# Two-layer perceiver block: seven block products for keys and values, and normalisation chains on VectorE

## The chip, the cores and the metric

The kernel runs on one core of one Trainium2 chip. The metric is the device time of one launch in microseconds. Lower is better. The time before is the median of three runs, 1554.78 us.

## The reference

Sixteen sequences of 64 tokens, 256 features each (x), pass through two layers of three blocks, each added to x after a layer norm. A context of 1024 rows a sequence feeds the cross-attentions.

```
x = x + cross_attention(layernorm(x), ctx_1024, mask, ...)          # layer 0, 16 heads of 16
x = x + attention over the 16 sequences, rotary, causal             # layer 0
x = x + mixture of 8 experts, top 2 (layernorm(x))                  # layer 0
x = x + cross_attention(layernorm(x), ctx_1024, bias, mask, ...)    # layer 1
x = x + attention over the 64 tokens, rotary (layernorm(x))         # layer 1
x = x + fp4_linear(silu(fp4_linear(h, gate)) * fp4_linear(h, up), down)   # layer 1, h = layernorm(x)
...
kv = context @ Wkv + bkv          # (1024 x 256) @ (256 x 512): keys, then values, of one sequence
attn = softmax(q k / 4, masked); out = attn @ v; out @ Wout + bout
...
fp4: per block of 16 elements scale = max|x| / 6, round x / scale to the fp4 grid, times scale
```

Everything is float32. The quantization of the feed-forward is done by adding and subtracting a large number of the right magnitude.

## The kernel before

Tokens lie in eight tiles of 128 rows (two sequences each), n = 0 to 7. The work goes by stages: the cross-attention of layer 0 (0 to about 530 us in the profile), the attention over sequences (to about 660), router and experts (to about 870), then layer 1, in which `cross_attention` runs again and its `after` hook starts, for each finished tile, `row_attention` and `feed_forward` as chains between the steps of the next tiles.

**Cross-attention.** The outer loop runs over 64 slots: 16 sequences b, two halves of the features dt, two halves of the keys hf. In slot i the kernel issues on PE, in this order: the scores of slot i + 2 (`scores`, L445: four matmuls of 512 columns on four row groups at once), the first part of the keys and values that are due (`project`, L361), the transposes of the exponentials of two key blocks (`transpose_keys`, L475), the second part of what is due, two more transposes, and the products with the values of slot i - 1 (`attend`, L489). VectorE adds the mask to the scores and takes their running minimum in one instruction (L456, with its read-out), ScalarE makes exponentials of 1024 columns at a time when both halves are there (L467). The transposes and products leave PSUM by copies: in odd slots by VectorE, in even ones by ScalarE (`evacuate`, L217 and L219; keys with their bias L378 and L380). In layer 1 half of the transposes of odd slots go to ScalarE too (L602).

`project` has eight steps a sequence: four for keys (L370: two matmuls of 512 columns, one for each half of the 256 contracted features), four for values (L385: four matmuls of 256 columns). Sequence b's steps are due in slots 4b - 4 to 4b - 1, two in each (L549). Every work tile in PSUM comes from one pool of seven banks (`bank`, L137, tile name psw), in turn; an eighth holds the outputs (pso).

PE's order is that of the program (`manual_schedule`). The other engines' order is set by the scheduler. Each engine runs its instructions in order. The chains (`queries`, `outputs`, and the later layers) are generators: each `yield` hands on to the next step of the slot, so that the number of yields sets how far a chain's steps lie apart in PE's order.

**Layer norm of a tile** (`layernorm_rows`, L241): statistics on VectorE, an inverse root by three Newton steps of three 128x1 operations each on GpSimd (L256 to L258), and the normalisation on GpSimd (L260). **Output projection** (`project_rows`, L297): VectorE adds the bias to PSUM (L303), GpSimd adds the result to x (L304).

**Quantization** (`fp4`, L883): absolute value on ScalarE (L890), block maximum, scale and reciprocal on VectorE (L893 to L898), product, exponent, addition and subtraction, product (L899 to L911). `feed_forward` (L1361) quantizes the normalised tile, multiplies by gate and up (L1376) in two halves of 352 columns, quantizes the two halves of h in turn, transposes (L1391) and multiplies by the down weights (L1405).

**Ahead of time.** While the middle stages run, PE fills gaps with the keys and values of layer 1 for nine sequences (`make_ahead`), from two buffers of the pool `ahead` (actx) and staging buffers (astage); the first two contexts are loaded on SP's queue with the later weights (`later`, L614). The feed-forward weights wgT, wuT, wdT (L1159) are filled during the experts' stage and are unused before.

Of the kernel before, what the change touches and what calls it, by code (L numbers as in the profile page):

```python
# [118 lines left out]
def kernel(ctx: ExitStack, tc: tile.TileContext, a: dict, out: bass.AP):  # L119
# [121 lines left out]
    def layernorm_rows(pool, n, name="xnr"):  # L241

        st = small.tile([P, 6], F32, name="bnst")
        nc.vector.bn_stats(st, x[n])
        mv = small.tile([P, 2], F32, name="mvr")
        nc.vector.bn_aggr(mv, st)
        va = small.tile([P, 1], F32, name="var")
        nc.vector.tensor_scalar(va, mv[:, 1:2], EPS, None, ALU.add)

        half = small.tile([P, 1], I32, name="half")  # L250
        nc.vector.tensor_scalar(half, va.bitcast(I32), 1, None, ALU.logical_shift_right)
        r = small.tile([P, 1], F32, name="rsd")
        nc.vector.tensor_scalar(r.bitcast(I32), half, -1.0, 1597463007.0, ALU.mult, ALU.add)
        t = small.tile([P, 1], F32, name="nwt")
        for _ in range(3):
            nc.gpsimd.tensor_scalar(t, r, va, r, ALU.mult, ALU.mult)  # L256
            nc.gpsimd.tensor_scalar(t, t, -0.5, 1.5, ALU.mult, ALU.add)
            nc.gpsimd.tensor_tensor(r, r, t, ALU.mult)  # L258
        xn = pool.tile([P, D], F32, name=name)
        made[name] = nc.gpsimd.tensor_scalar(xn, x[n], mv[:, 0:1], r, ALU.subtract, ALU.mult)  # L260
        yield
        yield
        yield
        return xn
# [32 lines left out]
    def project_rows(n, oT, w, bias):  # L297

        pm = bank()
        for c in range(KC):  # L300
            nc.tensor.matmul(pm[:, :D], oT[:, c, :], w[:, c, :], start=(c == 0), stop=(c == KC - 1))  # L301
        t = small.tile([P, D], F32, name="prow")
        nc.vector.tensor_tensor(t, pm[:, :D], bias, ALU.add)  # L303
        nc.gpsimd.tensor_tensor(x[n], x[n], t, ALU.add)  # L304


    def cross_attention(layer, wq, wkv, wo, bq, bk, bv, bo, mask, keep, bias, after, ready, arrive, idle):
        side = "right" if layer else "left"
        with ExitStack() as st:
# [83 lines left out]

            def queries(n):
# [3 lines left out]
                xn = yield from layernorm_rows(single, n, "xnq")  # L398
# [98 lines left out]
            def outputs(b):  # L497
# [38 lines left out]
                project_rows(n, oT, wo, rowbias(bo))  # L536
# [6 lines left out]
            for b in range(1, B):  # L543
                if b not in ready:
# [29 lines left out]
            with tc.manual_schedule(engines={mybir.EngineType.PE}):  # L574
# [15 lines left out]
                for i in range(len(slots) + 1):  # L590
# [5 lines left out]
                    for part in range(2):  # L596
                        for step in steps[part::2]:
                            project(*step, vector)
                        if i < len(slots):
                            b, dt, hf = slots[i]  # L600
                            for k in (4 * hf + 2 * part, 4 * hf + 2 * part + 1):
                                transpose_keys(b, dt, k, vector and (layer == 0 or part == 0))  # L602
                                advance()
# [7 lines left out]
                    if i % 4 == 0 and i // 4 + 2 < B:  # L611
                        load(i // 4 + 2)
                        if i == 4:
                            for w, source in later:  # L614
                                nc.sync.dma_start(w, source)
                            later.clear()
                    if i % 8 == 0 and i // 8 + 1 < NT:
# [54 lines left out]
    actx, ready = {}, {}  # L672
# [6 lines left out]
    for b in range(2):  # L679
        load_ahead(b, lambda w, source: later.append((w, source)))  # L680
# [202 lines left out]
    def fp4(pool, dst, src, rows, n, tag, most=None):  # L883

        nb = n // BLK
        most = most or n
        shape = [rows, nb, BLK]
        t = pool.tile([P, most], F32, name=f"t{tag}")[:rows, :n]
        t3 = t.rearrange("p (g k) -> p g k", k=BLK)
        nc.scalar.activation(t, src, AF.Abs)  # L890
        yield
        scl = pool.tile([P, most // BLK], F32, name=f"scl{tag}")[:rows, :nb]
        nc.vector.tensor_reduce(scl, t3, AX.X, ALU.max)  # L893
        nc.vector.tensor_scalar(scl, scl, 1.0 / 6.0, 1e-12, ALU.mult, ALU.max)
        rsc = pool.tile([P, most // BLK], F32, name=f"rsc{tag}")[:rows, :nb]
# [4 lines left out]
            t3, src.rearrange("p (g k) -> p g k", k=BLK), rsc.unsqueeze(2).to_broadcast(shape), ALU.mult  # L900
# [4 lines left out]
        m = pool.tile([P, most], F32, name=f"m{tag}")[:rows, :n]  # L905
# [257 lines left out]
    def quantize_weights(step, pool):  # L1163
        if step < 4:
# [9 lines left out]
            for _ in fp4(pool, q, raw, PG, n, "w"):  # L1174
# [12 lines left out]
        elif step < 6:  # L1187
# [4 lines left out]
            for _ in fp4(pool, q, raw, P, NI, "d"):  # L1192
# [15 lines left out]
    def last_layers(one):  # L1208
# [11 lines left out]
        def row_attention(n, two):  # L1220
            vz = vzs[n % 2]
            xn = yield from layernorm_rows(two, n)
# [134 lines left out]
            project_rows(n, oT, wproj, rowbias("L1_attn_b_proj"))  # L1357
# [3 lines left out]
        def feed_forward(n, two):  # L1361
            tok = slice(n * P, (n + 1) * P)
            xn = yield from layernorm_rows(two, n)
            yield from fp4(one, xn, xn, P, D, "h", NI)
# [5 lines left out]
            for g in range(2):  # L1370
                cols = slice(g * NH, (g + 1) * NH)
                pg = bank()[:, :NH]
                pu = bank()[:, :NH]
                for ps, w in ((pg, wgT), (pu, wuT)):
                    for c in range(KC):
                        nc.tensor.matmul(  # L1376
                            ps, xT[:, c, :], w[:, c, cols], start=(c == 0), stop=(c == KC - 1)
# [3 lines left out]
            yield  # L1381
            for g in range(2):
                cols = slice(g * NH, (g + 1) * NH)
                yield from fp4(one, h[:, cols], h[:, cols], P, NH, "h", NI)
            yield
            hT = one.tile([P, NCH, P], F32, name="hT")
            for g in range(0, NCH, 3):
# [12 lines left out]
            yield  # L1400
            yield
            py = bank()[:, :D]
            for j in range(NCH):
                w = min(P, NI - j * P)
                nc.tensor.matmul(py, hT[:w, j, :], wdT[:w, j, :], start=(j == 0), stop=(j == NCH - 1))  # L1405
# [107 lines left out]
```

## Time and profile before

| what | us |
|---|---|
| median of 3 runs | 1554.78 |
| lowest and highest run | 1544.31, 1555.05 |
| profiled execution | 1553.52 |
| its span, first to last instruction | 1551.8 |
| PE, VectorE, ScalarE, GpSimd busy | 1411.0, 880.4, 725.3, 285.4 |

The span is what the profile covers, and the 1.7 us beyond it lie around the first and last instruction. The profile names lines of the kernel above. A float32 matmul takes two passes on PE and shows as two records, a transpose shows as one. "x8" in a line is eight records. PEld is the load of the fixed operand of a matmul, which overlaps with PE. An operation's tile names stand as out<-in. The chain that ended last is followed back from the last instruction: each piece waits for the one before it.

### The profile page before, as it was taken

The page shows a single profiled execution, that of the slowest core. Times are in us where ns is not written, and L with a number is a line of the kernel's source. Part 1 is how long each engine was busy: PE and PEld are TensorE (multiplying, and loading weights), DVE is VectorE, ACT ScalarE, POOL GpSimd, SP SyncE. Part 2 cuts the span into 40 slices and gives each one's busy share as a digit, 9 for nine tenths or more (in the row PEclk, how much of TensorE's full clock was granted, in tenths as well). Part 3 has the DMA queues.
Part 4 walks back from the last instruction along what each step waited for, and adds up shares of the span by engine and source line. Part 5 has one row for each costly group of instructions (what it writes and reads, how often), then busy time and mean ns, then how long its engine had stood idle before and what let it go on. Part 6 is the DMA issues. An engine that isn't in the chain of part 4 may idle for free.

```text
span 1551.8 us, 32601 instructions
## 1 busy us (share of the span) xinstructions
PE 1411.0 (91%) x13488; PEld 995.0 (64%) x13488; DVE 880.4 (57%) x2325; ACT 725.3 (47%) x1339; POOL 285.4 (18%) x502
## 2 busy tenths in 40 slices
PE   4999999999999998999999787888899999999754
PEld 2667766676667655768887555565657666666542
DVE  2556665656565533365721265675767675757543
ACT  2555555555555532223221475564656465646321
POOL 4101010000000031013300134241414141311111
PEclk8999999999999999999999798888889999999876
DMA  8111110101000021377774232322101111100000
GB/s 281 59 31 35 32 59 32 35 32 59 31 28 2 35 90 70 105 260 235 234 283 147 90 117 94 118 86 74 57 14 46 46 52 49 42 5 1 5 5 3
DMA packets 53073, 119.48 MB, mean 77 GB/s; under 512 B 4877, under 2 KB 24333, under 8 KB 50621
## 3 DMA queue, kind: packets, MB, share of 16 engines
q1 hardware_dynamic: 48876, 109.93, 21.0%
q0 software_dynamic: 1648, 4.72, 1.1%
q10 hardware_dynamic: 2400, 2.76, 0.5%
q8 instruction: 106, 1.74, 0.5%
q14 instruction: 43, 0.34, 0.1%
HBM read 94.32 MB, written 23.07 MB: 76 GB/s over the span
## 4 chain that ended last, share of the span: by engine, by line
PE 73%; DVE 12%; POOL 4%; ACT 4%; DMA 3%; issue 3%; ACTq 0%; POOLq 0%; DVEq 0%; SPq 0%
PE psw L475 11%; PE psw L385 10%; PE psw L370 9%; PE psw L445 8%; PE pso L489 7%; PE psw L659 4%; PE psw L1085 4%; PE psw L1105 4%; DVE e L456 3%; PE psw L646 3%; ACT e L467 3%; PE psw L1376 2%; PE psw L1405 2%; PE psw L301 2%; DMA kd<-astage 1%
## 5 line engine op out<-in xcount | busy, mean ns | idle before, releaser
L467 ACT ACTIVATE e<-e,mn 128x1024 f32<-128x1024 f32 x256 | 291.1, 1139 | 125.3 <-DVE mn L456 125.3
L475 PEld LDWEIGHTS psw<-consts,e 128*128 128x128 f32 x2048 | 242.6, 144 | 111.6 <-issue 64.3
L475 PE MATMUL psw<-consts,e 128*128 128x128 f32 x2048 | 286.8, 280 | 10.1 <-DVE mn L456 5.7
L456 DVE CUSTOM_DVE_ANT_0 e<-psw,negb,mn 128x512 f32<-128x512 f32 x256 | 177.9, 747 | 180.0 <-PE psw L445 180.0
L456 DVE CUSTOM_DVE_ANT_0 e<-psw,negb 128x512 f32<-128x512 f32 x256 | 162.9, 686 | 87.0 <-PE psw L445 86.8
L219 ACT COPY eT<-psw 128x512 f32<-128x512 f32 x320 | 174.1, 590 | 58.3 <-PE psw L475 57.9
L445 PE MATMUL psw<-kT,qm 32*128 32x512 f32 x1024 | 167.7, 690 | 3.4 <-ACT qm L415 1.8
L489 PE MATMUL pso<-eT,v 128*32 128x128 f32 x4096 | 146.0, 286 | 0.0
L370 PE MATMUL psw<-ctxT,w_L_xattn_Wkv 128*128 128x512 f32 x256 | 125.0, 612 | 11.9 <-DMA ctxT<-in_ctxT_dram 11.9
L217 DVE COPY eT<-psw 128x512 f32<-128x512 f32 x192 | 123.0, 678 | 9.3 <-PE psw L475 9.3
L489 PEld LDWEIGHTS pso<-eT,v 128*32 128x32 f32 x4096 | 109.4, 114 | 28.0 <-issue 25.9
L385 PE MATMUL psw<-w_L_xattn_Wkv,ctxT 128*128 128x256 f32 x512 | 123.6, 385 | 0.0
L385 PEld LDWEIGHTS psw<-w_L_xattn_Wkv,ctxT 128*128 128x128 f32 x512 | 93.0, 190 | 33.7 <-issue 11.9
L370 PEld LDWEIGHTS psw<-ctxT,w_L_xattn_Wkv 128*128 128x128 f32 x256 | 44.3, 192 | 68.4 <-issue 55.1
L219 ACT COPY v<-psw 128x512 f32<-128x512 f32 x46 | 27.0, 588 | 123.8 <-PE psw L385 123.8
L304 POOL TENSOR_TENSOR x<-x,prow 128x256 f32<-128x256 f32 x24 | 17.4, 727 | 315.1 <-DVE prow L303 315.1
L659 PE MATMUL psw<-w_L_xattn_Wkv_w,actx 128*128 128x256 f32 x288 | 73.4, 409 | 0.8 <-ACT astage L653 0.8
L445 PEld LDWEIGHTS psw<-kT,qm 32*128 32x128 f32 x1024 | 49.2, 197 | 37.8 <-issue 20.2
L337 POOL TENSOR_SCALAR negb<-m 128x1024 f32<-128x1024 uint8 x16 | 16.7, 1046 | 285.8 <-DVE mn L456 172.4
L380 ACT ACTIVATE kT<-psw,colb 128x512 f32<-128x512 f32 x48 | 32.8, 687 | 75.3 <-PE psw L370 75.3
L646 PE MATMUL psw<-actx,w_L_xattn_Wkv_w 128*128 128x512 f32 x144 | 66.2, 599 | 1.3 <-DVE x L632 1.3
L659 PEld LDWEIGHTS psw<-w_L_xattn_Wkv_w,actx 128*128 128x128 f32 x288 | 58.0, 206 | 13.6 <-issue 3.8
(248 smaller groups left out, 1974.0 us busy)
## 6 DMA issues: line engine op xcount, KB each, us to landing
ctxT<-in_ctxT_dram SPq DMA_DIRECT2D x23, 1024.0 KB, 5.0
w<-in_L_ffn_w_dram SPq DMA_DIRECT2D x16, 1024.0 KB, 6.9
actx<-in_ctxT_dram SPq DMA_DIRECT2D x9, 1024.0 KB, 6.8
kd<-astage SPq DMA_DIRECT2D x36, 256.0 KB, 3.7
vd<-astage SPq DMA_DIRECT2D x36, 256.0 KB, 2.4
kT<-kd SPq DMA_DIRECT2D x9, 1024.0 KB, 6.1
v<-vd SPq DMA_DIRECT2D x9, 1024.0 KB, 5.0
ab<-in_fside_BxS_dram SPq DMA_DIRECT2D x32, 256.0 KB, 3.4
```

The source lines that it names most:

```text
L217: nc.vector.tensor_copy(dst, src)
L219: nc.scalar.copy(dst, src)
L370: nc.tensor.matmul(pm, wkv[:, c, dt * P : (dt + 1) * P], ctxT[b][:, c, cols], start=(c == 0), stop=(c == KC - 1),)
L385: nc.tensor.matmul(pm[:, j * D : (j + 1) * D], ctxT[b][:, c, (k + j) * P : (k + j + 1) * P], wkv[:, c, D : 2 * D], start=(c == 0), stop=(c ...
L445: nc.tensor.matmul(sc[g], qm[b // 2][r : r + 32, dt, b % 2, :, :].rearrange("p j q -> p (j q)"), kT[b][r : r + 32, dt, cols], start=True, ...
L456: nc.vector.tensor_tensor_reduce(out=e[:, cols], in0=sc[g], in1=negb[b][:, cols], scale=1.0, scalar=3e38 if hf == 0 else mn[b][:, 0, pr : ...
L467: nc.scalar.activation(e, e, AF.Exp, scale=-1.0, bias=mn[b][:, 1, pr : pr + 1], accum_out=sums[b][:, pr : pr + 1])
L475: nc.tensor.transpose(pt[:, g * P : (g + 1) * P], es[b, dt, g][:, k * P : (k + 1) * P], ident)
L489: nc.tensor.matmul(po[b][32 * g : 32 * g + 32, dt, :], v[b][:, k, pr * 32 : (pr + 1) * 32], e[:, g, :], start=(k == 0), stop=(k == NK - 1),)
L646: nc.tensor.matmul(pm, w1kv[:, c, dt * P : (dt + 1) * P], actx[b][:, c, cols], start=(c == 0), stop=(c == KC - 1),)
L659: nc.tensor.matmul(pm[:, j * D : (j + 1) * D], actx[b][:, c, (k + j) * P : (k + j + 1) * P], w1kv[:, c, D : 2 * D], start=(c == 0), stop=( ...
L1085: nc.tensor.matmul(ph[:, j * CAP : (j + 1) * CAP], w1[:, c, (f + j) * P : (f + j + 1) * P], xeT[:, c, :], start=(c == 0), stop=(c == KC - 1),)
```

## The change

It has two parts.

**Seven products for keys and values of layer 0**, from the third sequence on. The contracted features and the output features are each cut in two halves of 128, the 1024 keys in two halves of 512. Of the eight block products that a 2x2 by 2x2 block product takes, one is dropped by multiplying sums of blocks (the scheme of Strassen and Winograd). It is done once for keys (m = 0) and once for values (m = 1). Sums of weights are made once on GpSimd, in the space of wgT; sums of the context's blocks on GpSimd for each sequence, in the buffers actx (`sum_context`); the products are single matmuls without accumulation, of 512 columns for keys and four of 128 columns for values. Their sums are made while they leave PSUM: three VectorE operations in each of the two phases, and in the second phase two copies on ScalarE into the space of wdT and two additions on GpSimd. Partial sums lie in wuT and astage. Each phase of a sequence takes a slot, from slot 4b - 5 on: three products in the first, four in the second. Half of the transposes of odd slots now leave by ScalarE in layer 0 too. The two contexts for layer 1 are loaded at slot 59, since sums use their buffers.

**Chains on VectorE**, in layer 1: `layernorm_rows` of the row attention, of the feed-forward and of the first query does its Newton steps and normalisation on VectorE; the output bias is added to x earlier on GpSimd, so that `project_rows` is one VectorE addition; `fp4` takes the absolute value inside its maximum and so leaves ScalarE out (in the quantization of weights too); the feed-forward's halves are 384 and 320 columns, and in the last tile the second half of gate and up, the first half of the transposes and of the down product are interleaved with the quantizations.

```diff
+        if vector:
+            nc.vector.tensor_scalar(va, va, -0.5, None, ALU.mult)
+            for _ in range(3):
+                nc.vector.tensor_scalar(t, r, va, r, ALU.mult, ALU.mult)
+                nc.vector.scalar_tensor_tensor(r, t, 1.5, r, ALU.add, ALU.mult)
+            made[name] = nc.vector.tensor_scalar(xn, x[n], mv[:, 0:1], r, ALU.subtract, ALU.mult)
+            return xn
...
+        if bias is None:
+            nc.vector.tensor_tensor(x[n], pm[:, :D], x[n], ALU.add)
+            return
...
+            seven = layer == 0
+                wsum = wgT.rearrange("p c n -> p (c n)")[:, : 10 * P].rearrange("p (o m n) -> p o m n", o=5, m=2)
+                    nc.gpsimd.tensor_tensor(wsum[:, o, :, :], p0, p1, op)
+                nc.gpsimd.tensor_scalar(wsum[:, 4, :, :], w4[:, 1, :, 1, :], -1.0, 1.0, ALU.mult, ALU.mult)
...
+            def sum_context(b):
+                t = xsum[b] = ahead.tile([P, KC, SK], F32, name="actx").rearrange("p c (o k) -> p (c o) k", o=2)
+                X = ctxT[b]
+                for o, p0, p1 in (
+                    (0, X[:, 0, HK:], X[:, 0, :HK]),
+                    (1, X[:, 1, HK:], t[:, 0, :]),
+                    (2, X[:, 1, HK:], X[:, 0, HK:]),
+                    (3, t[:, 1, :], X[:, 1, :HK]),
+                ):
+                    nc.gpsimd.tensor_tensor(t[:, o, :], p0, p1, ALU.subtract)
...
+                def product(a_, x_):
+                    pm = bank()
+                    if m == 0:
+                        nc.tensor.matmul(pm, a_, x_, start=True, stop=True)
+                    else:
+                        for q in range(4):
+                            cols = slice(q * P, (q + 1) * P)
+                            nc.tensor.matmul(pm[:, cols], x_[:, cols], a_, start=True, stop=True)
...
+                if (phase, part) == (0, 0):
+                    nc.vector.tensor_copy(s1[b, m], product(W[:, 0, 0, :], X[:, 0, :HK]))
+                    p6 = product(wsum[:, 1, m, :], t[:, 1, :])
+                    nc.vector.tensor_tensor(u2[b, m], p6, s1[b, m], ALU.add)
+                elif (phase, part) == (0, 1):
+                    put(0, 0, product(W[:, 1, 0, :], X[:, 1, :HK]), s1[b, m])
+                elif (phase, part) == (1, 0):
+                    s5 = held[b, m] = ahead.tile([P, HK], F32, name="astage")
+                    p5 = product(wsum[:, 0, m, :], t[:, 0, :])
+                    nc.vector.tensor_tensor(s5, p5, u2[b, m], ALU.add)
+                    p7 = product(wsum[:, 2, m, :], t[:, 2, :])
+                    put(1, 1, p7, s5)
+                    nc.vector.tensor_tensor(u2[b, m], p7, u2[b, m], ALU.add)
+                else:
+                    put_far(0, 1, product(wsum[:, 3, m, :], X[:, 1, HK:]), held.pop((b, m)))
+                    put_far(1, 0, product(wsum[:, 4, m, :], t[:, 3, :]), u2[b, m])
...
+                if seven and b >= 2:
+                            due.setdefault(4 * b - 5 + 2 * m + phase, []).append((b, m, phase))
...
-                                transpose_keys(b, dt, k, vector and (layer == 0 or part == 0))
+                                transpose_keys(b, dt, k, vector and part == 0)
...
-        nc.scalar.activation(t, src, AF.Abs)
-        nc.vector.tensor_reduce(scl, t3, AX.X, ALU.max)
+        nc.vector.tensor_reduce(scl, s3, AX.X, ALU.max, apply_absolute_value=True)
...
+            if alone:
+                hidden(halves[0])
+                first = fp4(tiles, h[:, halves[0]], h[:, halves[0]], P, 3 * P)
+                next(first)
+                hidden(halves[1])
+                for _ in first:
+                    pass
+                turn_hidden(0)
+                py = bank()[:, :D]
+                down(0)
+                for _ in fp4(tiles, h[:, halves[1]], h[:, halves[1]], P, NI - 3 * P, 3 * P):
+                    pass
+                turn_hidden(3)
+                down(3)
```

In the diff, `put` adds a PSUM bank and a partial sum into keys (with their bias) or values on VectorE, and `put_far` copies the bank on ScalarE into wdT and adds there on GpSimd.

## The prediction

> **What bounds the kernel now.** I read the stage table first (windows of the trace; columns: stretch, its length, busy PE, weight loads, VectorE, ScalarE, GpSimd, each with a count of instructions, then granted clock, DMA share and GB/s).
>
> ```profile
> 40.00:510.00 470.00, 470.00 (x4213) 324.91 (x4211) 294.26 (x751) 254.30 (x471) 33.58 (x54) 1.00 0.11 36
> 870.00:1160.00 290.00, 245.87 (x2512) 165.98 (x2513) 185.74 (x535) 168.68 (x322) 84.84 (x148) 0.84 0.23 76
> 1160.00:1450.00 290.00, 281.38 (x2656) 198.90 (x2654) 198.79 (x553) 167.86 (x319) 75.14 (x141) 0.99 0.11 34
> 1450.00:1552.00 102.00, 53.15 (x515) 36.70 (x514) 41.05 (x110) 19.16 (x37) 14.49 (x36) 0.73 0.01 5
> ```
>
> The first row is the first cross-attention: PE never stops, VectorE is busy 63%, ScalarE 54%, GpSimd 7%. There a PE column saved is time saved, as long as nothing else comes to set the pace. The last row is the opposite: no engine is busy more than 52%, so the end is a chain of dependent steps.
>
> PE's order of time in the first stretch (start, length, engine, line, tiles, count of passes; a float32 matmul that isn't a transpose shows as two) prices the columns. I go by start to start, since ends are modelled:
>
> ```profile
> 306.96 1.99 PE L385 MATMUL psw<-w_L_xattn_Wkv,ctxT 128*128 128x256 f32 x8
> 308.79 1.04 PE L475 MATMUL psw<-consts,e 128*128 128x128 f32 x8
> ...
> 325.26 1.06 PE L405 MATMUL psw<-xTq,w_L_xattn_Wq 128*128 128x128 f32 x8
> 326.15 0.60 PE L475 MATMUL psw<-consts,e 128*128 128x128 f32 x4
> ```
>
> A step of values (four matmuls of 256 columns) takes 1.83 us just after scores and 1.73 elsewhere, so 0.433 a matmul; a step of keys (two of 512) likewise 1.82 and 1.72, so 0.86. Four matmuls of 128 columns, each with its own 128x128 weights (L405), take 0.89 us, so 0.2225.
>
> The chain that ended last shows the tail: sum on GpSimd, nine tiny GpSimd operations, normalisation on GpSimd, the absolute value on ScalarE, then quantization.
>
> ```profile
> 1513.90 0.73 POOL x L304
> 1514.66 0.44 DVE bnst L244
> ...
> 1518.90 1.29 POOLq L1509
> 1520.21 0.42 ACT th L890
> ...
> 1525.62 6.37 PE psw L1376 x12
> 1532.01 0.46 ACT h L1379
> ...
> 1542.34 1.12 PE psw L1391 x4
> 1543.45 5.21 PE psw L1405 x12
> ```
>
> **Part 1: seven products (batches 2 to 15 of layer 0).** Per batch, before: two key steps at 1.82 and two at 1.72 = 7.08; values the same with 1.83 and 1.73 = 7.12; together 14.20 us. After: keys 7 x 0.86 + 0.2 (two blocks that follow scores) = 6.22; values 28 x 0.2225 + 0.2 = 6.43; together 12.65. Saved 1.55 us a batch, 21.7 us in 14 batches.
>
> One rule of the Trainium skill speaks against this, for values become 28 matmuls of 128 columns in place of 16 of 256. TensorE: Matmul & The Clock Gate, section Back-to-back issue gap, gives about 81 ns for a pair of weight load and matmul at 128 columns and 131 at 512: a narrow matmul costs 0.62 of a wide one, not a quarter. Scaled to this kernel's 0.43 us pass of 512, 56 passes would take 56 x 0.62 x 0.43 = 14.9 us a batch against 7.1 now, a loss of 7.8 x 14 = 109 us. The row says 0.111 us a pass at 128 columns, 0.26 of a wide one, in this kernel, with new weights each time: the loads fit behind the float32 passes. I take the row.
>
> **What the sums cost elsewhere.** VectorE, per batch: 12 operations on 128x512 from PSUM where 4 were. Nearest rows: the plain copy 0.68, the one with a bias 0.75 (L378), the 128x256 sum of PSUM and SBUF 0.42 (L303), which scales to 0.68 or so. New: 10 x 0.68 + 2 x 0.75 = 8.3; gone: 2 x 0.75 + 2 x 0.69 = 2.9 and four score copies (now on ScalarE) 2.7. Net +2.7: from 294.26/470 x 31.2 = 19.5 us to 22.2 in a batch of 29.65 (31.2 is the period of the batches in the chain), 75%. ScalarE: +4 x 0.59, its four evacuations as before: 16.9 to 19.3, 65%. GpSimd: eight sums of 128x512, which neither VectorE nor PE waits for by more than a slot; L343 is that form, 1.30 us each with VectorE at 66%: +10.4 on 2.2, 42%. The block sums of the context are made two to three slots (about 20 us) ahead of their first product, and those that end in keys or values are wanted at least two slots later. Thus totals fit; order within a slot is what can hurt.
>
> **The bank ring.** Seven work banks (psw) turn round, for scores, products and transposes alike. A slot had ten; it has 11 (odd, three products) or 12 (even, four), and one more with a transposed output. Walk through an odd slot: PE 1.07 scores + 1.82 two products + 0.87 transposes + 0.96 third product + 0.87 + 1.01 attend = 6.6 us, on average 0.3 more for queries and outputs. VectorE starts its masked minima 1.16 after the slot (314.23 to 315.39 in the trace), ends them at 3.85, the first copy at 4.5, the sum at 5.15, two score copies at 6.4, with an output 7.0, third sum 7.7. The next slot's fourth scores want the bank of the second score copy (6.4), or with outputs between, that of the outputs (7.0) or the third sum (7.7). PE is there at 6.6 to 7.1. So the wait is 0 to 0.6 in an odd slot. I take 0.2 in each of the two odd slots of a batch: 14 x 0.43 = 6 us; none (0) below, and 1.8 a batch (25 us: PE waits 0.9 in every odd slot, for the third sum and the reciprocal and oT that stand about it) above. In even slots VectorE is through at 5.7, PE at 7.5: covered. PE stays above 95% busy, where the trace had clock 0.99 (1160 to 1450). Layer 0: 21.7 - 6 = 15.7 us.
>
> **Start, weights sums, moved loads.** Five GpSimd operations on weights (about 4 x 0.73 + 0.8 = 3.7 us) stand ahead of the first Newton step. GpSimd idles from 7.4 to 13.6 and again 2.3 us before 17.6; weights are there by 11.9, when PE starts. I take 0; up to 3 if that cover is gone. Two 1 MB loads for the later keys move on SP's queue from 25 us to slot 59, some 35 us ahead of their use, 6.8 us each: 0. Should they be late, the filling after the last scores shifts by as much.
>
> **Part 2: chains on VectorE (layer 1).** From the last VectorE step of a normalisation to its end GpSimd takes 1464.28 to 1468.50 = 4.2 us; on VectorE seven operations of about 0.2 (L894, 128 partitions x 22: 0.18) and one of 128x256 (0.56, L234): 2.0. Saved 2.2. The hop to GpSimd for x (0.74 + gaps) goes: 0.8. The absolute value: 0.45. So 3.4 for feed-forward and 3.0 for row attention. On the tail's path lie tile 6's feed-forward, tile 7's row attention and tile 7's feed-forward: 9.8. Then the last tile's halves. Before: 1525.62 to 1548.66 = 23.0. After: first 384 columns of gate and up 6.37 x 384/704 = 3.5; silu 0.5; VectorE back to back 9.6 (two products with h of 0.5, two quantizations of 4.3); transposes and evacuation of the second half 1.1; half of the down matmul 2.6: 17.3. Saved 5.7. Sum 15.5; tile 7's row attention also waits for tile 6's work, so I take 14 (9 if only the last feed-forward counts, 18 if clocks rise with fewer gaps).
>
> In the 580 us before, VectorE gets 16 x 2.0 = 32 us of work, 5% more, but loses waits for GpSimd and ScalarE at the head of its queue. PE there waits 15.6 us for xnq and xnr from GpSimd, 18.0 for outputs from VectorE. I take 3 us of gain (12 of gain, 8 of loss).
>
> **Sum.** 15.7 + 14 + 3 = 32.7. Span 1551.8 - 32.7 = 1519.1. The profiled execution lasted 1553.52, 1.7 around its span, and lies 1.3 below the median of 1554.78: 1522.
>
> **Rivals.**
> *The ring eats layer 0* (0.18): the upper end above, 25 us against 21.7 saved; with the 17 of layer 1: 1541, from 1533 to 1549. For it: work banks are the one resource that the change asks more of. Against it: odd slots before carried 2.7 + 2.7 + 1.4 of VectorE work, and no wait shows.
> *VectorE's sums hold PE up, slower* (0.08): the sums, which read PSUM and SBUF, cost what GpSimd's do (1.30) because the two engines hold each other up. In an odd slot the second score copy then ends at 3.85 + 2.6 + 1.28 = 7.7 and the third sum at 9.6, 8.7 on average, where PE comes at 6.85: 1.8 x 28 odd slots = 51 us lost, 21.7 and 17 saved: 1567. It decides from 1.4 us of wait a slot (38.7/28), which is a sum of about 1.13 us. For it: GpSimd goes from 7% to 42% busy. Against it: SBUF — State Buffer, section SBUF: two separate sides, ties the exclusive hold on VectorE's side to two SBUF inputs or a two-port mode, and these have one input in PSUM; and L456, which also reads PSUM and SBUF, took 0.66 us with its read-out (159.11 us in 240) where GpSimd was 7% busy and 0.67 (96.34 in 144) where it was 29%.
> *More than forecast* (0.11): no ring waits, 12 us from the freed queues: 1554.8 - 21.7 - 12 - 15.5 = 1505.
> *The change does not shorten PE's work* (inside the first rival): narrow matmuls cost more than 0.2225.
>
> **Chances.** The forecast 0.63 (own range 1508 to 1536). 1% of 1554.78 is 15.5 us, about what a measurement here can tell from nothing: faster is below 1539. The ring case lies astride it, 0.08 and 0.10. Faster 0.63 + 0.11 + 0.08 = 0.82, same 0.10, slower 0.08. Eight in ten: 1503 to 1544.
>
> **What would show it.** Right: batches 29.7 to 30.2 us apart in layer 0, PE at 98% or more, eight values passes in 0.89 us, VectorE 75% and GpSimd 42%, the tail 14 us shorter. Wrong: PE waiting for VectorE sums ahead of scores, sums far above 0.7 us, a granted clock below 1.00 there, PE waiting for context sums, or a tail that still ends in the same 23 us.

## The result, and the profile after

The changed kernel takes 1551.8 us (median of 20 runs, 1547.5 to 1556.0); the kernel before, run on the same chip beside it, 1544.3 (20 runs, 1539.1 to 1555.1). The ratio is 1.004, with a 95% interval of 1.0025 to 1.0056: 7.5 us slower by the medians (3.9 to 8.6 by the interval) where 32.7 less had been forecast. The profiled execution of before (1553.5) is among the longest of its kernel, so the two profiles, 1551.8 and 1550.0 us of span, don't show the loss in their totals. Below, totals are compared by medians, and stretches by profiles.

The stage table of the changed kernel (length, busy PE, weight loads, VectorE, ScalarE and GpSimd, granted clock, DMA share, GB/s):

```profile
40.00:510.00 470.00, 460.11 (x4581) 332.62 (x4583) 331.43 (x812) 286.36 (x536) 173.83 (x166) 1.00 0.12 41
870.00:1160.00 290.00, 235.71 (x2526) 163.20 (x2526) 191.68 (x588) 169.88 (x320) 66.14 (x91) 0.88 0.22 76
1160.00:1450.00 290.00, 270.94 (x2491) 192.78 (x2493) 192.51 (x571) 150.65 (x280) 44.33 (x65) 0.96 0.10 32
1450.00:1550.00 100.00, 66.94 (x670) 47.18 (x662) 56.14 (x166) 27.45 (x53) 5.63 (x7) 0.81 0.02 5
```

PE, never idle in the first row before, now stands still for 9.9 us of it. In the second and third rows PE lost some 10 us of busy time each at much the same length: it waits there. PE does more in the last row, 67% where it was 52%, but that is in part work which came later: slot 124 (slots are explained below) starts at 1429.8 us where it started at 1410.5.

To place the time exactly I take the start of the first masked minimum of a slot from VectorE's order of time. Slots are numbered through both cross-attentions: 0 to 63 are layer 0, 64 to 127 layer 1.

| stretch | before, us | after, us | after - before |
|---|---|---|---|
| start to slot 8 | 89.5 | 93.3 | +3.8 |
| slots 8 to 60, layer 0 | 404.9 | 399.5 | -5.4 |
| slots 60 to 64 (column attention, MoE) | 383.5 | 381.9 | -1.6 |
| slots 64 to 124, layer 1 | 532.6 | 555.1 | +22.5 |
| slot 124 to the end | 141.2 | 120.2 | -21.1 |

Profiles with the same work differ by some 3 us in the first and the last two rows and by up to 7.7 in the third (last section). The forecast had -15.7 for layer 0, -3 for slots 64 to 124, and -14 for the end.

**The loss in layer 1.** PE's longest waits for normalised rows between 870 and 1450 us, before and then after (line, what it waited for: sum in us, times, longest):

```profile
PE psw L269 <- POOL xnq L260: 12.0, 4, 3.6
```

```profile
PE psw L276 <- POOL xnq L267: 38.9, 7, 8.1
PE psw L276 <- DVE xnr L261: 12.1, 3, 5.5
```

L276 is the transposes of normalised rows, `xnq` the rows of the next query tile. One of the seven places in PE's order of time, after:

```profile
1179.29 0.60 PE L583 MATMUL psw<-consts,e 128*128 128x128 f32 x4
1184.89 0.69 PE L276 MATMUL psw<-consts,xnq 128*128 128x128 f32 x2 [5.01 <-POOL xnq L267]
1185.38 1.06 PE L583 MATMUL psw<-consts,e 128*128 128x128 f32 x4
```

PE's order is written out by hand and lets nothing pass: the other four transposes of exponentials (L583) stand behind. VectorE's queue shortly ahead of this wait:

```profile
1173.27 0.48 DVE L1035 TENSOR_TENSOR h<-th,sclh 128x320 f32<-128x320 f32 x1
1173.66 0.15 DVE L260 SCALAR_TENSOR_TENSOR rsd<-nwt,rsd 128x1 f32<-128x1 f32 x1
...
1174.86 0.41 DVE L261 TENSOR_SCALAR xnr<-x,mvr,rsd 128x256 f32<-128x256 f32 x1
1175.18 0.48 DVE L1261 SCALAR_TENSOR_TENSOR x<-g,rt_w,x 128x256 f32<-128x256 f32 x1
1175.58 0.75 DVE L564 CUSTOM_DVE_ANT_0 e<-psw,negb,mn 128x512 f32<-128x512 f32 x1
...
1180.37 0.15 DVE L253 TENSOR_SCALAR rsd<-half 128x1 int32<-128x1 int32 x1
```

and GpSimd's:

```profile
1180.64 0.34 POOL L264 TENSOR_SCALAR nwt<-rsd,var 128x1 f32<-128x1 f32 x1 [4.38 <-DVE rsd L253]
...
1183.62 1.22 POOL L267 TENSOR_SCALAR xnq<-x,mvr,rsd 128x256 f32<-128x256 f32 x1
```

The query's rows are complete only after both gathered rows are added (L1261), and these additions now come behind row attention's Newton steps (L259, L260) and the second quantization of a feed-forward (its last step is L1035), and are threaded among masked minima and copies. The last statistic (L253) is done at 1180.5. Then the query's own Newton steps, left on GpSimd, take another 4.2 us. In the kernel before, the same additions started 6.3 us after the slot's first masked minimum (1170.38, slot 100 at 1164.09) and the statistics were done at 8.5; now they start at 11.9 (slot 100 at 1163.28) and end at 17.2. The same place in the kernel before, where quantization (L893) comes behind the statistics:

```profile
1170.38 0.99 DVE L1137 SCALAR_TENSOR_TENSOR x<-g,rt_w,x 128x256 f32<-128x256 f32 x2
...
1172.46 0.15 DVE L253 TENSOR_SCALAR rsd<-half 128x1 int32<-128x1 int32 x1
...
1175.03 0.52 DVE L893 TENSOR_REDUCE sclh<-th 128x22 f32<-128x352 f32 x1 [1.41 <-ACT th L890]
```

**The gain in layer 0.** Prices are as forecast, in PE's order of time (start to start, eight passes of values 0.89 and 1.00, two of keys 0.87):

```profile
319.38 1.02 PE L444 MATMUL psw<-ctxT,w_L_xattn_Wkv 128*128 128x512 f32 x2
320.25 0.60 PE L583 MATMUL psw<-consts,e 128*128 128x128 f32 x4
...
332.26 1.16 PE L448 MATMUL psw<-w_L_xattn_Wkv,ctxT 128*128 128x128 f32 x8
333.26 1.06 PE L448 MATMUL psw<-wgT,actx 128*128 128x128 f32 x8
334.15 1.04 PE L583 MATMUL psw<-consts,e 128*128 128x128 f32 x8
```

The rule of the Trainium skill that the prediction set against this (TensorE: Matmul & The Clock Gate, section Back-to-back issue gap, with a narrow matmul at 0.62 of a wide one, and 109 us lost by the prediction's estimate) differs from the measurement, which decides: eight passes in 0.89 us against two in 0.87, or 0.26. What was not foreseen is one wait in every second batch, always of 1.3 us, for the scaled outputs:

```profile
364.95 1.04 PE L583 MATMUL psw<-consts,e 128*128 128x128 f32 x8
367.32 0.41 PE L635 MATMUL psw<-consts,osb 128*128 128x128 f32 x2 [1.33 <-DVE osb L622]
```

```profile
364.68 0.69 DVE L486 TENSOR_TENSOR wuT<-psw,astage 128x512 f32<-128x512 f32 x1
365.29 1.28 DVE L217 COPY eT<-psw 128x512 f32<-128x512 f32 x2
366.58 0.59 DVE L622 TENSOR_TENSOR osb<-psw,rec 64x128 f32<-64x128 f32 x2
```

Outputs are ready for scaling at 364.1, when PE has gone on from their transposes (L619), but stand behind a block sum (L486) and two copies on VectorE; the transposes of the result are PE's next step.

The ring of banks holds PE up too. The list of waits does not show it, since it falls inside a group of matmuls. Scores after an odd slot, before and then after:

```profile
368.29 1.14 PE L445 MATMUL psw<-kT,qm 32*128 32x512 f32 x8
369.36 1.99 PE L385 MATMUL psw<-w_L_xattn_Wkv,ctxT 128*128 128x256 f32 x8
```

```profile
322.44 1.54 PE L553 MATMUL psw<-kT,qm 32*128 32x512 f32 x8
323.91 1.98 PE L444 MATMUL psw<-actx,wgT 128*128 128x512 f32 x4
```

```profile
322.06 0.74 DVE L463 SCALAR_TENSOR_TENSOR kT<-psw,colb,astage 128x512 f32<-128x512 f32 x1
```

In the kernel before, the four matmuls of a slot's scores start within 0.02 us, and PE's next step follows 1.07 us after the first. Here the fourth starts 0.40 us behind the third, 0.06 us after the end of the slot's third sum on VectorE (L463, 322.80), whose semaphore it waits for since that sum frees its bank; the next step follows after 1.47. In two batches this happens once, and a second time with 0.22 us: 0.31 us a batch.

**The end.** The chain that ended last, after, from the last tile's sum:

```profile
1519.73 0.43 DVE x L310
...
1523.01 0.42 DVE xnr L261
...
1528.34 6.58 PE psw L1507 x16
...
1546.93 0.42 DVE prow L1568
```

From the sum behind the projection (L310, L303 before) to gate and up 8.6 us where it was 12.2, and from there to the last sum 18.6 where it was 23.1.

### The profile page after: what moved, and what is told of

Same layout as the page of the kernel before. It is cut to its first block, busy times and chain, and to the rows that moved or that the text cites. A ratio compares the mean times of both kernels' runs of the same rounds, so it can differ in the third digit from the quotient of the medians.

```text
span 1550.0 us, 33551 instructions
## 1 busy us (share of the span) xinstructions
PE 1389.2 (90%) x13796; PEld 998.2 (64%) x13796; DVE 928.9 (60%) x2509; ACT 745.7 (48%) x1373; POOL 366.2 (24%) x449
## 3 DMA queue, kind: packets, MB, share of 16 engines
q1 hardware_dynamic: 48876, 109.93, 20.9%
## 4 chain that ended last, share of the span: by engine, by line
PE 72%; DVE 15%; ACT 5%; DMA 3%; issue 3%; POOL 2%; ACTq 0%; SPq 0%; DVEq 0%; POOLq 0%
PE psw L583 11%; PE psw L553 9%; PE pso L597 7%; PE psw L444 6%; DVE e L564 5%; PE psw L448 5%; PE psw L1209 4%; ACT e L575 4%; PE psw L1229 4%; PE psw L778 3%; PE psw L380 3%; PE psw L765 3%; PE psw L395 2%; PE psw L1507 2%; PE psw L1356 1%
## 5 line engine op out<-in xcount | busy, mean ns | idle before, releaser
L583 PEld LDWEIGHTS psw<-consts,e 128*128 128x128 f32 x2048 | 240.6, 144 | 97.8 <-issue 55.4
L583 PE MATMUL psw<-consts,e 128*128 128x128 f32 x2048 | 284.5, 279 | 7.7 <-ACT e L575 5.2
L219 ACT COPY eT<-psw 128x512 f32<-128x512 f32 x384 | 208.1, 587 | 148.7 <-PE psw L583 148.4
L597 PE MATMUL pso<-eT,v 128*32 128x128 f32 x4096 | 139.0, 277 | 0.0
L217 DVE COPY eT<-psw 128x512 f32<-128x512 f32 x128 | 82.4, 682 | 3.1 <-PE psw L583 3.1
L772 ACT ACTIVATE astage<-psw,colb 128x512 f32<-128x512 f32 x36 | 24.7, 687 | 77.2 <-PE psw L765 45.3
L448 PEld LDWEIGHTS psw<-wgT,actx 128*128 128x128 f32 x448 | 53.3, 192 | 10.6 <-issue 5.3
L448 PE MATMUL psw<-wgT,actx 128*128 128x128 f32 x448 | 58.3, 278 | 0.0
L1209 PE MATMUL psw<-xeT,w 128*128 128x256 f32 x256 | 56.6, 379 | 0.8 <-ACT astage L772 0.8
L1229 PE MATMUL psw<-w,hT 128*128 128x256 f32 x256 | 56.6, 379 | 0.0
L395 PE MATMUL psw<-w_L_xattn_Wkv_w,ctxT 128*128 128x256 f32 x224 | 54.8, 387 | 1.9 <-DVE mn L564 1.9
L444 PE MATMUL psw<-actx,wgT 128*128 128x512 f32 x112 | 56.4, 605 | 0.0
```

Source lines behind the costliest of these rows:

```text
L219: nc.scalar.copy(dst, src)
L444: nc.tensor.matmul(pm, a_, x_, start=True, stop=True)
L448: nc.tensor.matmul(pm[:, cols], x_[:, cols], a_, start=True, stop=True)
L583: nc.tensor.transpose(pt[:, g * P : (g + 1) * P], es[b, dt, g][:, k * P : (k + 1) * P], ident)
L597: nc.tensor.matmul(po[b][32 * g : 32 * g + 32, dt, :], v[b][:, k, pr * 32 : (pr + 1) * 32], e[:, g, :], start=(k == 0), stop=(k == NK - 1),)
L1209: nc.tensor.matmul(ph[:, j * CAP : (j + 1) * CAP], w1[:, c, (f + j) * P : (f + j + 1) * P], xeT[:, c, :], start=(c == 0), stop=(c == KC - 1),)
```

## The experiments

All times are medians beside runs of the kernel before on the same chip; the ratio to before has its 95% interval. The theory: the change loses time at places where PE, in fixed order, waits for something that stands later in VectorE's queue, in layer 1 for the query's statistics (38.9 us), in layer 0 for the scaled outputs (9.3 us). The rivals: VectorE simply carries too much, the bank ring, and the price of products and sums. Runs with different parts were not all made on one chip, so each is best compared by its ratio to the kernel before beside it.

**Each part alone (e1, e2).** e1 is the kernel before with part 1 (the lines of `seven`, `project_seven`, `sum_context`, the due times, the split of copies, the moved loads), e2 the kernel before with all the rest of the diff.

> Seven products alone, layer 1 as before. Theory (layer 0 gains little since PE waits there, layer 1 loses by the moved chains): batches of layer 0 still 30.7 us apart, layer 1 starts some 3 us earlier, everything behind as before: 1541 us against 1544 (1538 to 1543). The prediction's step would give 1544 - 15.7 = 1529. Rival (sums and narrow products are what costs the time): 1550 or more.

Measured: 1547.5 (before 1548.3), ratio 0.9992 (0.9973 to 1.0011). Slots 8 to 60 took 399.46 us, 5.5 less than before; PE's waits for outputs were 9.3 us, as in the changed kernel. The median is above the 1538 to 1543 expected: the interval allows at most 4 us of gain.

> Chains on VectorE alone, eight products as before. Theory: the middle of layer 1 loses about 22 us, the end gains about 21: 1546 (1542 to 1550), with PE waiting 4 to 8 us per tile at the transposes of the normalised queries. The prediction's step would give 1544 - 17 = 1527. Rival (the seven products cost the time): 1525 to 1530, no such waits.

Measured: 1555.8, ratio 1.0062 (1.0041 to 1.0084), above the range. Slots 64 to 124 took 555.4 us, the end 119.7, and PE waited:

```profile
PE psw L276 <- POOL xnq L267: 38.9, 7, 8.1
```

So the chains alone make the wait in layer 1, to the tenth of a microsecond, and alone make the kernel slower. The seven products are neither the loss nor much of a gain.

**The queries' transposes later (e3, e6).** In `queries`, on top of the changed kernel (e3) and of the kernel before (e6):

```
+                if layer and n:
+                    yield
+                    yield
+                    yield
                 xT = transposed_rows(single, xn, "xTq")
```

> The changed kernel, with the transposes of the normalised queries of layer 1 put three quarter slots (about 6 us) later in PE's order; no work added or taken, VectorE's load the same. Theory (the next query's statistics come late out of VectorE's queue and PE, in fixed order, stands at their transposes): most of the 39 us of such waits goes, 1527 to 1535. Rival (VectorE simply carries too much there): the wait turns up at the next thing that comes from VectorE, 1548 to 1553.

Measured: 1511.3 us, ratio 0.9771 (0.9749 to 0.9793), 16 us below the best that was expected. The row for xnq is gone from the waits, which begin with

```profile
PE psw L276 <- DVE xnr L261: 12.1, 3, 5.5
```

Slots 64 to 124 take 514.8 us where the changed kernel took 555.1: 40.3 us, about the 38.9 of waits. Nothing was taken off VectorE, so its load was not the cause.

> The kernel before, with only the transposes of the queries of layer 1 put three quarter slots later. Theory (the change itself made the 39 us of waits there; before it had 12): about 12 us less than before, 1533 to 1537. Rival (the later transposes alone bring the 37 us, with or without the change): 1507 to 1515.

Measured: 1537.2 us, ratio 0.9941 (0.9921 to 0.996), 9 us less by the ratio (6 to 12). Slots 64 to 124 take 516.9 us. The rival falls: most of e3's gain is a wait that the change had made (in the profiles slots 64 to 124 give 15.7 us here, 40.3 in e3). Once nobody waits for queries, the chains' own worth there would be 514.8 - 516.9 = -2.1 us; profiles with the same work differ by as much (2.5 us between e5 and e12 below), so no worth is shown.

**What stands ahead of the query (e7, e8).** The diff does two things to the chains: they run on VectorE, and, since pauses (`yield`) went with the steps on GpSimd and ScalarE, their parts come earlier in the hand-written order (four quarter slots at gate and up). The second is not in the list of changes above, nor in the prediction. e7 puts the parts of tiles 0 to 5 back, e8 puts the Newton steps of those tiles back on GpSimd and leaves the order.

```
e7: +   if n < NT - 2: yield          # row attention, once
    +   if n < NT - 2: yield x3       # feed-forward, ahead of the first quantization
    and one yield per quantization of h, none between the halves of gate and up, and of the transposes
e8: layernorm_rows(two, n, "xnr", n >= NT - 2), without its three yields for n < NT - 2
```

> The changed kernel, with the parts of row attention and feed-forward of tiles 0 to 5 put back to the quarter slots of the kernel before; their chains stay on VectorE. Theory A (the feed-forward now comes a slot earlier in the order, and its quantization stands in VectorE's queue ahead of the next query's statistics): waits at the queries' transposes back to some 12 us, 1520 to 1535. Theory B (the Newton steps on VectorE are what stands ahead): waits stay, 1545 to 1555.

> The changed kernel, with the Newton steps and normalisations of tiles 0 to 5 back on GpSimd and the order of all engines' work otherwise that of the changed kernel. Theory A (the place of the feed-forward): 1548 to 1560, waits at the queries' transposes stay and those at the rows' grow by some 2 us each. Theory B (the Newton steps on VectorE): 1520 to 1535.

Measured: e7 1519.7 us (ratio 0.9816, 0.978 to 0.9852), slots 64 to 124 in 519.1. e8 1540.3 us (0.9958, 0.9941 to 0.9975), 546.4. Waits of e7, then e8:

```profile
PE psw L276 <- POOL xnq L267: 17.6, 4, 8.6
```

```profile
PE psw L277 <- POOL xnq L267: 22.5, 7, 4.1
PE psw L277 <- POOL xnr L267: 16.1, 6, 5.2
```

Putting the order back recovers 36.0 of the 40.3 us with every Newton step still on VectorE: theory A. Putting the Newton steps back recovers 8.7 us, which neither theory had: it shortens the queries' wait by 16 us, but rows that come slowly from GpSimd now cost 16 where those from VectorE had cost 12. Both stand ahead of the query, and the earlier place in the order is the larger. What the parts moved in VectorE's queue is set by a scheduler from the order of the program, so e7 can't tell the feed-forward from row attention.

**Layer 0: outputs or bank ring (e4, e12).** e4 is the changed kernel with two more yields in `outputs` ahead of the transposes of `osb` (L635), layer 0 only. e12 is the version with both moves (e5, below), with two of the eight copies of scores of an odd slot taken from ScalarE back to VectorE:

```
-  transpose_keys(b, dt, k, vector and part == 0)
+  transpose_keys(b, dt, k, vector and (layer == 0 or part == 0))
```

> The changed kernel, with the transposes of the scaled outputs of layer 0 put half a slot later in PE's order. Theory (PE waits 1.3 us there once per two batches): 7 x 1.3 = 9 us less, 1543. Rival (the ring of banks sets the pace, and the wait at the outputs is only where it shows): less than 3 us, 1549 to 1552.

Measured: 1544.8 us, ratio 0.9977 (0.9958 to 0.9997); slots 8 to 60 take 390.66 us, 8.8 less than the changed kernel, and no wait for `osb` is left in layer 0. The wait was its own cause, but for a small part: in every second batch the fourth score now waits 0.36 us more for its bank.

> The version with both moves (1505 us), with two more of the eight copies of scores of each odd slot of layer 0 on VectorE instead of ScalarE, as the kernel before had them: 28 x 2 x 0.68 = 38 us more work for VectorE there. By the walk of the prediction VectorE then ends an odd slot at 9.0 us where PE comes at 7.1: 1.9 x 28 = 53 us, 1558. Rival (VectorE has room, and the ring does not set the pace): 1505 to 1510.

Measured: 1504.1 us (e5: 1505.1), slots 8 to 60 in 391.04 us against 390.67. 38 us more work on VectorE cost 0.4 us. My expectation was 53 us off: it took the end of VectorE's work in the slot for what PE waits for. The two copies come behind the third sum and behind the outputs' scaling in VectorE's queue, and the fourth score waits for one of these two: 0.40, 0.36 and 0.20 us in three slots of eight, in e5 and in e12 alike.

**Both moves (e5).**

> The changed kernel with both moves: transposes of the queries of layer 1 three quarter slots later, transposes of the scaled outputs of layer 0 half a slot later. Theory (two separate waits of PE): 1511 - 9 = 1502 (1498 to 1507). Rival (what layer 0 saves is lost again before the end): 1511.

Measured: 1505.1 us, ratio 0.972 (0.9684 to 0.9755), 38 to 49 us faster than before by the interval, and faster than both kernels; of the 9 us expected over e3, 6 show in the medians and 8.8 in slots 8 to 60. Its stage table:

```profile
40.00:500.00 460.00, 459.40 (x4575) 332.04 (x4573) 331.55 (x811) 286.30 (x536) 173.81 (x166) 1.00 0.13 41
870.00:1160.00 290.00, 256.69 (x2736) 179.69 (x2733) 211.77 (x655) 180.10 (x338) 73.62 (x106) 0.93 0.24 81
1160.00:1400.00 240.00, 234.60 (x2223) 164.43 (x2222) 169.85 (x498) 135.73 (x255) 36.97 (x51) 1.00 0.10 33
```

PE is 99.9% and 97.8% busy in the first and third rows with VectorE at 72% and 71%, as loaded as in the changed kernel or more.

**A Newton chain that nobody waits for (e11).** The queries of tiles 1 to 7 normalise on VectorE too (`layernorm_rows(single, n, "xnq", layer == 1)`), at the same place in PE's order (three more `yield`, since the steps on GpSimd brought three).

> The version with both moves (1505 us), the Newton steps of the queries of tiles 1 to 7 on VectorE too, their transposes at the same place in PE's order. Theory (a chain on VectorE costs nothing where nobody waits for what stands behind it): 1505 (1502 to 1508). Rival (each of these chains holds up the masked minima or the copies behind it, about 2 us each): 1515 to 1520.

Measured: 1503.8 us (0.9721, 0.9687 to 0.9754): no cost that can be measured.

**What the end is made of (e9, e10, e13 to e17).** Each takes one thing from e5. e9: `alone = False`. e10: tiles 6 and 7 normalise on GpSimd, order kept. e13: the yields of e7, for tiles 6 and 7. e14: the absolute value by ScalarE ahead of the maximum. e15: `project_rows` with its bias and GpSimd's sum in layer 1, as before. e16 is e10 and e13 together, e17 is e10, e14 and e15 together.

> The version with both moves (1505 us), its last feed-forward in one piece as those of the other tiles. The prediction counted 5.7 us for the halves: 1511. Rival 1 (the extra gain of the end, 21 against 14, comes from the halves): 1516 to 1518. Rival 2 (the halves bring nothing): 1505.

> The version with both moves (1505 us), the Newton steps and normalisations of tiles 6 and 7 on GpSimd. The prediction counted three chains of 2.2 us on the way to the end: 1511 to 1512. Rival 1 (only the last of them counts): 1507. Rival 2 (the extra gain of the end comes from here): 1517 or more.

> The version with both moves (1505 us), the parts of row attention and feed-forward of tiles 6 and 7 put back to the quarter slots of the kernel before, their chains still on VectorE. Theory (what the end gained beyond the chains is that gate and up of tile 6 no longer stand behind tile 7's normalised rows in PE's order): 8 to 12 us more, 1513 to 1517. Rival (the order brings nothing, the chains all of it): 1503 to 1507.

> The version with both moves (1505 us), the absolute values of the feed-forwards' quantizations on ScalarE again. The prediction counted 0.45 for each quantization of normalised rows on the way to the end; with those of h there are four to six: 1507 to 1508. Rival (the extra gain of the end comes from here): 1511 or more.

> The version with both moves (1505 us), the sums of projections and rows in layer 1 in two steps again, the second on GpSimd. The prediction counted 0.8 for each of three on the way to the end: 1507 to 1508. Rival (the extra gain of the end, or of the middle, comes from here): 1511 or more.

| kernel | median, us | ratio to before | slots 64 to 124 | slot 124 to the end |
|---|---|---|---|---|
| e5 | 1505.1 | 0.972 (0.9684 to 0.9755) | 514.7 | 121.6 |
| e11, the end as in e5 | 1503.8 | 0.9721 (0.9687 to 0.9754) | 515.7 | 118.5 |
| e9, no halves | 1504.0 | 0.9718 (0.9686 to 0.975) | 514.9 | 120.5 |
| e10, Newton | 1507.8 | 0.9729 (0.9693 to 0.9765) | 517.8 | 122.0 |
| e13, order | 1508.3 | 0.9733 (0.9695 to 0.9772) | 514.8 | 122.0 |
| e14, absolute value | 1505.7 | 0.9718 (0.9681 to 0.9754) | 511.8 | 121.6 |
| e15, sums | 1512.2 | 0.9756 (0.9718 to 0.9794) | 519.7 | 123.9 |
| e16, order and Newton | 1516.2 | 0.9783 (0.9752 to 0.9814) | 513.5 | 129.0 |
| e17, Newton, absolute value, sums | 1514.8 | 0.9775 (0.9744 to 0.9806) | 515.6 | 127.8 |

e5's own profile is long at the end. e12, with the same work there, took 121.6 us too, but e3 and e11, again with the same work, 118.5. The last gate and up took 7.68 us in e5, at a granted clock of 0.65, and 6.44 in e11, at 0.77; of the other 1.9 us, 1.3 lie ahead of it and 0.6 behind. In e15 it took 7.86, at 0.63. So I set the parts against 118.5: without halves 2.0 us more, Newton steps 3.5, order 3.5, absolute values 3.1, sums 5.4 (1.4 of it the clock). None of them is the one source of the end's gain, which is 22.7 us against 118.5. The medians of e9, e10, e13 and e14 lie within 3.2 us of e5's; e15 is 7 above, 5.6 by the ratios, whose intervals overlap. Hence the pairs:

> The version with both moves (1505 us), with the places of tiles 6 and 7 in PE's order as before and their Newton steps on GpSimd, both at once; alone each cost 2 to 3 us. Theory (the place costs only where the chain is slow: gate and up of tile 6 then stand behind tile 7's slow normalisation): more than their sum, the stretch from slot 124 to the end 128 to 134 us where it was 122 with each alone, 1513 to 1518. Rival (the parts add): 124 us, 1509 to 1511.

> The version with both moves (1505 us), with Newton steps of tiles 6 and 7, absolute values and sums of projections all on GpSimd and ScalarE again, the order and the halves kept; alone they cost 3, 0 and 7 us (the last 5 of them in the middle). Theory (the chains themselves are a third of the end's gain): slot 124 to the end 126 to 129 us, 1514 to 1518. Rival (the parts do not add because another path takes over at 122 us): 122 to 124 us, 1510 to 1512.

e16's end takes 129.0 us, 10.6 more than 118.5, where order and Newton steps alone came to 3.5 each: the place costs more where the chain is slow. The chain that ended last in e5 and in e16, at gate and up of tile 6 (L1514, L1522):

```profile
1439.14 0.69 PE psw L276 x2
1439.83 1.71 PE psw L308 x4
1441.54 6.58 PE psw L1514 x16
1448.12 0.23 PE psw L276 x2
```

```profile
1435.73 2.09 PE psw L309 x4
...
1443.26 1.23 POOL xnr L267
1444.54 0.69 PE psw L277 x2
1445.23 7.30 PE psw L1522 x16
```

In e5 the transposes of tile 7's rows come after tile 6's gate and up; in e16, as in the kernel before, gate and up stand behind them, and they behind tile 7's projection (L309) and its Newton steps on GpSimd. e17, order kept, takes 127.8, 9.3 more than 118.5 and not more than its parts together (12.0). So two groups of parts, with the Newton steps in both, give back 10.6 and 9.3 us of the 22.7; how they and the rest add up to the whole was not tried.

## Why the prediction was wrong, step by step

*PE's price of the products: right.* 0.87 for a keys product, 0.89 and 1.00 for values, so 1.55 us saved in a batch. With the wait for outputs removed (e4, e5) slots 8 to 60, 13 batches, are 14.3 us shorter, 1.10 a batch, and the forecast with its 0.43 of waits was 1.12.

*VectorE's and GpSimd's sums: right in price, and cover.* Block sums on VectorE took 0.69 (L486, L492) and with a bias 0.75 (L463); on GpSimd 1.27 to 1.29, forecast 1.30, with GpSimd 37% busy (42 forecast) and VectorE 71% (75). The rival with sums of 1.30 on VectorE did not happen.

*The bank ring: right, and beside it a wait put at nothing.* It was to cost 0.43 us a batch where the fourth scores want a bank that the outputs or the third sum hold. It cost 0.31 in the changed kernel and 0.48 (0.96 in two batches) in e4 and e5, behind just these two. What the forecast lacked is PE's wait at L635 for VectorE's `osb`: 0.67 of the 1.13 us a batch that layer 0 fell short (1.55 - 0.42). The walk through the slot had that step as work of VectorE, not as something for which PE stands still.

*Start and moved loads: 0 forecast.* Slot 8 came 3.8 us later in the profile, but in others with the same work 1.5 to 4.7 later, and up to 2.8 without part 1 (e6). What is common to all with seven products, some 1.5, fits the first products of batch 2, due one slot earlier than the old steps were; this was not separated.

*Layer 1 between: the step that failed.* "VectorE gets 16 x 2.0 = 32 us of work, 5% more, but loses waits for GpSimd and ScalarE at the head of its queue" and "I take 3 us of gain (12 of gain, 8 of loss)" (the two terms make 4). Instead 22.5 us were lost. Load was the wrong measure: e3 took nothing off VectorE and won 40.3. A part of a chain takes a place in VectorE's queue, and with fewer pauses an earlier place, ahead of statistics for which PE stands still: 38.9 us at the queries' rows. The earlier place, of which the prediction says nothing, is the larger (e7 wins back 36.0 us, the Newton steps alone in e8 8.7). The prediction had a line that pointed there in hand, 15.6 us of PE's waits for xnq and xnr in the kernel before, and counted it as something to gain. It did not ask who is queued behind the moved instructions on VectorE, and who waits for that one.

*The end: 21 us, 14 forecast, and from other parts.* The halves were to bring 5.7. From gate and up to the end it is 23.5 us in before, 20.9 in e9 without halves, and 18.9 in e11 with them (20.7 in e5, at its lower clock): 2.0 for the halves, and 2.6 from the rest. ScalarE's absolute values fit that (e14 has them again, and takes 2.0 longer there than e11). No more than that for the halves shows in the medians either. Three chains of 3.0 to 3.4 were added up as if in a row; the order of tiles 6 and 7, which took one of them off the path (e16), was not looked at.

*The rivals.* None was this. The one that ends slower had a mechanism in layer 0 that didn't occur; the ring cost what the forecast itself had set down for it. The sum, -32.7, failed by 40.2 against the median; e3 and e4 show that two places of three and two quarter slots in a list of calls hold 47 us between them (1551.8 to 1505.1).

## What to carry to other kernels

When a chain is moved to another engine's queue, list what comes behind it there and whether the engine with the fixed order waits for one of these; a free share of busy time says nothing of that. A pause taken out of a generator moves everything behind it in the order, and on the other engines too: look at the order of all queues of the changed kernel, above all for a consumer whose place did not move while its producer's did. If PE waits for a late producer, first try the consumer some quarter slots later: here it was worth 40 us and cost nothing.

## What the runs showed of the hardware

VectorE took 38 us more work in 391 us of layer 0 with PE at its limit for 0.4 us, since it came behind what PE's fourth scores wait for (e12 against e5). A wait of 0.2 to 0.4 us inside a group of matmuls does not stand among the profile's waits; it shows in the distance from one group's start to the next (1.47 us for 1.07).

Stretches repeat very unequally. Slots 8 to 60 took 390.64 to 390.69 us in all ten kernels with the later outputs but the same copies. Slots 60 to 64, whose work the experiments on the changed kernel did not touch, took 378.2 to 385.9. Slots 64 to 124 came out 2.5 us apart for the same work (e5 and e12), the end 3.1 (e3 and e5), and the start to slot 8 2.8 (e6 against before). Why was not found; in the end part of it is the granted clock of the last gate and up, 0.65 or 0.77 (e5 and e9), for 1.3 us. A gain of a few microseconds is thus to be read from its own stretch, beside a second profile with the same work in that stretch.
